# Second product and transposes over 64 rows at a time between the scores of places 2 and 3

## The chip, the cores and the metric

The kernel runs on one core of one Trainium2 chip. A core has a matrix engine (TensorE: PE, its weight loads are shown as PEld), a vector engine (VectorE: DVE), an activation engine (ScalarE: ACT), a general engine (GpSimd: POOL) and a queue for transfers (SyncE: SP). Each works through its own instructions in order, and they wait for each other by semaphores. TensorE reads from the on-chip memory SBUF and writes to PSUM, which here serves as 8 banks of 128 partitions by 512 fp32 numbers.

The metric is the device time of one execution in microseconds (us), as a median over several executions. The kernel before: 1874.29 us, the median of 3 runs (1870.79 to 1875.33).

## The reference

The input is `x`, 16 batches of 512 rows by 256 features, fp32. Each row is normalised to `xn`, and two branches are computed from it and multiplied:

```python
v  = xn @ v_w + v_b                                   # 16 heads of 16 features
scores = table[i - j] + qm[i] + km[j] + 0.15 * (qc[i] . kc[j]) / sqrt(8)   # per head, causal
ctx = softmax(scores) @ v
h   = layernorm(xn + ctx @ out_w + out_b)
s   = layernorm(h + gelu(h @ ffn_w1 + ffn_b1) @ ffn_w2 + ffn_b2)     # 256 -> 1024 -> 256
hid = silu(fp4(xn) @ fp4(w_gate).T) * (fp4(xn) @ fp4(w_up).T)        # 256 -> 704
g   = silu(fp4(hid) @ fp4(w_down).T)                                 # 704 -> 256
out = x + s * g
```

`fp4` rounds blocks of 16 numbers to a scale times one of eight magnitudes. `table` depends on the batch and the head and comes from a small network over the mean of `xn`.

## The kernel before, in words

Everything is fp32; the scores and two rows of biases are in the kind fp32r, which TensorE takes in one pass. An fp32 product appears in the profile as two instructions, each with a weight load of its own.

**Steps.** The main loop (L1112) has 64 steps: 16 batches, four groups of four heads each. The group is the *place* of a step within its batch, 0 to 3. At a step the kernel computes the attention weights of group g of batch b, and beside them a quarter of the rest of the previous batch ("old"): places 0 and 1 have the output product of the attention (`output`, L530) and the first normalisation, places 1 and 2 at their end the first product of the feed-forward network (`expand`, L592: for one half of the batch's rows, 8 blocks f), places 2 and 3 its second product (`contract`, L603) for the two halves. Each step also turns and multiplies one tile of 128 rows of the fp4 branch (`turned_x`, `hidden`, `turned_hidden`, `gate`), and places 3 and 0 project the batch that comes next.

**Scores.** For a group the scores are computed twice. `maxima` (L427) computes them with rows of the softmax on the partitions and VectorE takes the maximum of each row under the causal mask (tile names `ms`, `junk`, `mx`). One step later `weights` (L466) computes them turned, with the negated maxima as two further rows of the operand, and ScalarE takes `Exp` (names `ws`, `pr`); then POOL multiplies by the table (`tabled`, L494), and one step later still `context` (L502) multiplies by the values (name `cp`). Both kinds of scores have 36 or 38 rows to sum over. Two heads stand at partitions 0 and 64, and their products are issued in pairs, one over the lower 64 rows of TensorE and one over the upper 64 (`scores`, L413). A group's causal blocks come in five bursts (`BURSTS`, L281): of 512 columns per bank, and from the third on of 384 + 128, 384 + 128 and 256 + 256.

**Banks.** The 8 banks of PSUM are three pools: one bank for `cp`; one pair of banks, tag `ws`, for the weights of a burst and, later in the step, for the second half of the gated products (`gu`); and five banks, tag `mm`, for everything else, handed out by `bank(name)` (L246) and free again when their last reader has ended. A burst of maxima takes two of the five until VectorE has read them. A burst of weights takes the pair until ScalarE's `Exp` has read it; where the plan says V it takes two of the five instead.

**Order.** TensorE's order is the order of the program; VectorE's and ScalarE's too, from the main loop on (`fixed`, L1111). Within a step it is set by a string for each place, `PLAN` (L711). W and V are bursts of weights, M a burst of maxima on TensorE, `!` the reading of the outstanding maxima by VectorE together with whatever stands in the list `later`; a small letter takes the next piece of a generator: f two products (of 8 blocks of 128 features, for two tiles of 128 rows) of the second feed-forward product, x the transposes of a tile of `xn` after rounding, y those of the rounded hidden tile (six blocks, in two pieces), h those of a half of `h` for the next `expand`. At places 2 and 3 the strings are

```python
"WVM!ffWMM!ffxWM!ffWM!ffyyh", "WMV!ffWMM!ffxWM!fffWM!yfy"
```

After the string come `gp`, `up` (L657, two of the five banks), the transpose of the maxima (`mp`), `gu` on the pair, then at place 2 `gate` (`dp`) and `expand`, at place 3 the values of the next batch (`vp`) and `gate`. `context` of the next step follows.

**The pieces that the change touches.** `biased` (L285) starts an accumulation with the bias row: a product of ones with the row, 128 rows, two tiles of 256 columns. `contract` (L603) accumulates 2 x 8 products of 128 rows on it in one bank; when the last has been issued, `added` is put into `later`, by which VectorE adds the bank to `h` and takes the statistics. `turned_h` (L583), `turned_x` (L646) and `turned_hidden` (L683) turn blocks of 128 x 128 into banks of the five, and ScalarE copies them to SBUF.

Of the kernel before, what the change touches and what calls it, by code (L numbers as in the profile page):

```python
# [12 lines left out]
F32 = mybir.dt.float32  # L13
# [15 lines left out]
P = 128  # L29
# [21 lines left out]
def tile_block(ctx: ExitStack, tc: tile.TileContext, a: dict, pos: bass.AP, win: bass.AP, out: bass.AP):  # L51
# [230 lines left out]
        ((0, 0, 0),), ((1, 0, 0),), ((0, 1, 0), (0, 3, 384)), ((1, 1, 0), (1, 3, 384)), ((0, 2, 0), (1, 2, 256))  # L282
    )

    def biased(acc, i, tiles=2):  # L285

        mm(
            acc[:, : tiles * D].rearrange("p (t d) -> p t d", t=tiles), sums,
            rows[:, i, :].unsqueeze(1).to_broadcast([P, tiles, D]),
            start=True, stop=False, skip_group_check=True,  # L290
        )

    def rows_of(tiles, t):
# [228 lines left out]
    def added(h, tiles, acc, mv):  # L522
# [4 lines left out]
        for t in tiles:  # L527
            statistics(mv[:, t, :], rows_of(h, t))

    def output(b, h, cts, half, mv):  # L530

        cTs, ops = {}, []

        def normal(t):
            tp = bank(f"ctp_{b}_{t}").rearrange("p (h s) -> p h s", s=SLOT)
            for g in range(H // 4):
                turn(tp[:, 4 * g : 4 * g + 4, :].rearrange("p h s -> p (h s)"), cts[g][:, t * P : (t + 1) * P])
            rinv = sb.tile([P, H], F32, name=f"rinv_{b}_{t}", tag="rinv", bufs=2)
            dve.reciprocal(rinv, tp[:, :, HD])
            cx = sb.tile([P, H, HD], F32, name=f"cx_{b}_{t}", tag="cx", bufs=3)  # L540
            dve.tensor_tensor(cx, tp[:, :, 0:HD], rinv.unsqueeze(2).to_broadcast([P, H, HD]), ALU.mult)
            return cx.rearrange("p h d -> p (h d)")

        def turned(t, cx):
            t2 = bank(f"ct2_{b}_{t}")
            for c in range(NC):
                turn(t2[:, c * P : (c + 1) * P], cx[:, c * P : (c + 1) * P])
            cTs[t] = sb.tile([P, D], F32, name=f"cT_{b}_{t}", tag="cx", bufs=3)
            act.copy(cTs[t], t2[:, :D])

        def product(t):
            acc = bank(f"op_{b}_{t}")
            op = acc[:, :D]
            biased(acc, 0, 1)
            cT = cTs[t]
            for c in range(NC):
                mm(op, cT[:, c * P : (c + 1) * P], wo[:, c, :], start=False, stop=(c == NC - 1), skip_group_check=True)
            later.append(lambda: added(h, (t,), acc, mv))

        first, second = 2 * half, 2 * half + 1  # L560
        cx = normal(first)
        yield 0.43
        cx2 = normal(second)
        yield 0.43
        turned(first, cx)
        yield 0.21
        turned(second, cx2)
        yield 0.21
        product(first)
        yield 0.96  # L570
        product(second)
        yield 0.96
# [7 lines left out]
            layernorm(rows_of(h, t), mv[:, t, 0:1], rs[:, i : i + 1], g1, b1)  # L580
            yield

    def turned_h(b, h, half):  # L583
        hT = sb.tile([P, NC, 2 * P], F32, name=f"hT_{b}_{half}", tag="hT")
        tp = bank(f"htp_{b}_{half}")
        for c in range(NC):
            for t in range(2):
                turn(tp[:, (2 * c + t) * P : (2 * c + t + 1) * P], rows_of(h, 2 * half + t)[:, c * P : (c + 1) * P])
        act.copy(hT.rearrange("p c t -> p (c t)"), tp)
        return hT  # L590
# [9 lines left out]
            act.activation(acts[f], fp[:, : 2 * P], AF.Gelu, bias=fb1[:, f : f + 1])  # L600
        return acts

    def contract(b, h, half, acts, mv, together=2):  # L603

        for first in range(2 * half, 2 * half + 2, together):
            tiles = tuple(range(first, first + together))
            acc = bank(f"f2_{b}_{first}")
            biased(acc, 1, together)
            for i, t in enumerate(tiles):
                at = (t % 2) * P  # L610
                for f in range(NF):
                    mm(
                        acc[:, i * D : (i + 1) * D], acts[f][:, at : at + P], w2[:, f, :],
                        start=False, stop=(f == NF - 1), skip_group_check=True,
                    )
                    if t == tiles[-1] and f == NF - 1:
                        later.append(lambda tiles=tiles, acc=acc: added(h, tiles, acc, mv))
                    if f % 2:
                        yield 0.88

    def finish(b, h, half, mv, gated):

# [20 lines left out]
        src = xns[b][t // 2].rearrange("p t d -> p (t d)")  # L643
        return xq, fp4_stages(xq.rearrange("p t d -> p (t d)"), src, P, 2 * D)

    def turned_x(b, t, xq):  # L646
        xq = xq[:, t % 2, :]
        tp = bank(f"xqtp_{b}_{t}")
        for c in range(NC):
            turn(tp[:, c * P : (c + 1) * P], xq[:, c * P : (c + 1) * P])  # L650
        xqTs[b, t] = sb.tile([P, D], F32, name=f"xqT_{b}_{t}", tag="xqT")
        act.copy(xqTs[b, t], tp[:, :D])
        yield 0.21
# [26 lines left out]

        return hid, halves(), fp4_stages(hid[:, :I_FF], hid[:, :I_FF], P, I_FF, ROUNDING[t])

    def turned_hidden(b, t, hq):  # L683
        hqT = sb.tile([P, NI, P], F32, name=f"hqT_{b}_{t}", tag="hqT")
        for first, count in ((0, 4), (4, 2)):
            tp = bank(f"hqtp_{b}_{t}_{first}")
            for i in range(count):
                turn(tp[:, i * P : (i + 1) * P], hq[:, (first + i) * P : (first + i + 1) * P])
            act.copy(hqT[:, first : first + count, :].rearrange("p i t -> p (i t)"), tp[:, : count * P])
            hqTs[b, t] = hqT  # L690
            yield 0.43 if first == 0 else 0.21
# [16 lines left out]
        ("r|px|rpp|p|yyr", "pp"),  # L708
        ("p|x||yytt|tt", ""),
    )  # L710
    PLAN = ("WMc!llWM!xWM!ccllyWMlyW!M!l", "WMll!kWM!lWM!xllyhWMccy!WM!l", "WVM!ffWMM!ffxWM!ffWM!ffyyh", "WMV!ffWMM!ffxWM!fffWM!yfy")  # L711

    def keeping(b, g):
        kept(b, g)
        yield 0.0

    def turning_h(b, half):
        turned_hs[half] = turned_h(b, xns[b], half)
        yield 0.43

    def take(pieces, count):
# [390 lines left out]
    for s in range(STEPS):  # L1112
# [11 lines left out]
        if has_old:  # L1124
            if g % 2 == 0:
                mv = sb.tile([P, NT, 2], F32, name=f"mv{1 + g // 2}_{old}", tag=f"mv{1 + g // 2}")
            hand = {
                "c": coming,
                "l": output(old, xns[old], cts[:4], g, mv) if g < 2 else None,
                "k": keeping(b, 0) if g == 1 else None,  # L1130
                "f": contract(old, xns[old], g - 2, acts[g - 2], mv) if g > 1 else None,
                "x": turned_x(b, g, xqs[s // 2]),
                "y": turned_hidden(*before, hq),
                "h": turning_h(old, g - 1) if g in (1, 2) else None,
            }
            plan = PLAN[g].split("|")
        else:
            if g == 0:
                coming = project(1, x_second)
            hand = {  # L1140
                **first_hand, "c": coming, "x": turned_x(b, g, xqs[s // 2]),
                "y": turned_hidden(*before, hq) if g > 0 else None,
            }
            plan = FIRST_PLAN[g][0].split("|")
# [97 lines left out]
    for half in range(2):  # L1242
        acts[half] = expand(old, half, hT)
        if half == 0:
            hT = turned_h(old, h, 1)
        for i, _ in enumerate(contract(old, h, half, acts[half], mv, 1)):
            if i % 4 < 3:
                continue
            caught_up()
            t = 2 * half + i // 4  # L1250
            rs = sb.tile([P, 2], F32, name=f"rs_last_{t}", tag="rs2")
            inverse_deviation(rs[:, :1], mv[:, t : t + 1, 1])
            layernorm(rows_of(h, t), mv[:, t, 0:1], rs[:, :1], g2, b2)
# [47 lines left out]
```

## Time and profile before

| what | value |
|---|---|
| median of 3 runs | 1874.29 us |
| profiled execution: span from the first to the last instruction | 1872.6 us |
| PE busy / weight loads busy | 1774.8 / 1240.5 us (95% / 66%) |
| DVE, POOL, ACT busy | 1423.1, 1310.3, 1069.1 us (76%, 70%, 57%) |
| mean granted TensorE clock | 0.973 |
| instructions on PE | 10411 |

The page gives no other time of the profiled execution than its span; the median of the runs is 1.7 us above it. After the first two batches the steps repeat: each batch takes the same 106.1 us, 29.2 at place 2, 24.4 at place 3, 24.0 at place 0 and 28.5 at place 1.

"Busy" of PE counts each instruction from its start to a modelled end and includes what the engine needs between instructions. The chain of work that ended last gives each instruction only the time until the next link begins, so the price of a piece is better read there. Times such as 953.95 are microseconds from the start of the span; the batch quoted throughout runs from 922.48 (context at place 2) to 1028.60.

### The profile page before, as it was taken

The page shows a single profiled execution, that of the slowest core. Times are in us where ns is not written, and L with a number is a line of the kernel's source. Part 1 is how long each engine was busy: PE and PEld are TensorE (multiplying, and loading weights), DVE is VectorE, ACT ScalarE, POOL GpSimd, SP SyncE. Part 2 cuts the span into 40 slices and gives each one's busy share as a digit, 9 for nine tenths or more (in the row PEclk, how much of TensorE's full clock was granted, in tenths as well). Part 3 has the DMA queues.
Part 4 walks back from the last instruction along what each step waited for, and adds up shares of the span by engine and source line. Part 5 has one row for each costly group of instructions (what it writes and reads, how often), then busy time and mean ns, then how long its engine had stood idle before and what let it go on. Part 6 is the DMA issues. An engine that isn't in the chain of part 4 may idle for free.

```text
span 1872.6 us, 31762 instructions
## 1 busy us (share of the span) xinstructions
PE 1774.8 (95%) x10411; PEld 1240.5 (66%) x10411; DVE 1423.1 (76%) x3887; ACT 1069.1 (57%) x1853; POOL 1310.3 (70%) x1128
## 2 busy tenths in 40 slices
PE   5679799999999999999999999999999999999998
PEld 2235467676776767676776767677676767677676
DVE  5878587787878777787878777787878778787754
ACT  5654455655665555556565565556555565565553
POOL 5467477767776776777676776777677776777671
PEclk8869799999999999999999999999999999999999
DMA  6344242432323242422334242332333242232200
GB/s 203 95 148 134 81 129 68 138 87 88 109 89 120 68 126 80 137 84 76 112 95 127 60 135 81 117 101 76 112 94 109 73 138 86 77 108 79 72 21 12
DMA packets 127114, 184.68 MB, mean 99 GB/s; under 512 B 15315, under 2 KB 57749, under 8 KB 126949
## 3 DMA queue, kind: packets, MB, share of 16 engines
q1 hardware_dynamic: 122496, 181.25, 32.2%
q8 instruction: 83, 1.36, 0.3%
q10 hardware_dynamic: 4004, 0.98, 0.3%
q14 instruction: 83, 0.67, 0.1%
q0 software_dynamic: 448, 0.42, 0.1%
HBM read 136.45 MB, written 45.09 MB: 97 GB/s over the span
## 4 chain that ended last, share of the span: by engine, by line
PE 81%; DVE 8%; POOL 1%; issue 1%; ACT 1%; DMA 0%; DVEq 0%; POOLq 0%; ACTq 0%
PE f L72 25%; PE dp L72 8%; PE gu L72 8%; PE cp L72 7%; PE ws L72 5%; DVE junk L72 4%; PE op L72 4%; PE gp L72 4%; PE up L72 4%; PE ms L72 4%; PE vp L72 3%; PE hqtp L72 2%; DVE cx L72 1%; PE qk_wk L72 1%; PE qk_wq L72 1%
## 5 line engine op out<-in xcount | busy, mean ns | idle before, releaser
L500 POOL TENSOR_TENSOR pr<-pr,table 128x1024 f32<-128x1024 f32 (+2 forms) x448 | 768.0, 1748 | 75.2 <-ACT pr L72 73.0
L72 DVE CUSTOM_DVE_ANT_0 junk<-ms,mask 128x512 bf16<-128x512 f32 (+3 forms) x1024 | 501.9, 490 | 231.9 <-PE ms L72 155.0
L72 ACT ACTIVATE pr<-ws 128x1024 f32<-128x1024 f32 (+1 forms) x350 | 327.0, 955 | 134.4 <-PE ws L72 129.1
L72 ACT ACT_TABLE_LOAD x168 | 215.5, 1283 | 64.3 <-PE gp L72 48.8
L72 PE MATMUL f<-w,act 128*128 128x256 f32 x1024 | 249.0, 387 | 0.0
L72 PE MATMUL f<-hT,w 128*128 128x256 f32 x1024 | 226.3, 380 | 0.0
L72 PEld LDWEIGHTS f<-hT,w 128*128 128x128 f32 x1024 | 194.8, 190 | 26.3 <-ACT hT L72 0.2
L72 PEld LDWEIGHTS f<-w,act 128*128 128x128 f32 x1024 | 187.0, 190 | 31.3
L232 POOL TENSOR_TENSOR wide<-wide,scale 128x704 f32<-128x704 f32 (+1 forms) x71 | 96.6, 1361 | 136.5 <-DVE wide L72 132.9
L72 PE MATMUL ws<-qT,kT 38*128 38x512 f32 (+3 forms) x1024 | 157.5, 371 | 21.4 <-ACT pr L72 16.5
L72 PE MATMUL dp<-wdT,hqT 128*128 128x256 f32 x768 | 176.2, 379 | 0.0
L72 PEld LDWEIGHTS dp<-wdT,hqT 128*128 128x128 f32 x768 | 146.1, 190 | 31.1 <-issue 6.7
L72 ACT ACTIVATE act<-f,fb 128x256 f32<-128x256 f32 x256 | 118.2, 474 | 75.3 <-PE f L72 72.5
L72 PE MATMUL ms<-kT,qT 36*128 36x512 f32 (+3 forms) x1024 | 145.1, 330 | 9.5 <-DMA kT<-k_d 6.3
L72 PE MATMUL cp<-pr,va 128*17 128x512 f32 (+3 forms) x2048 | 151.5, 434 | 0.0
L72 PEld LDWEIGHTS ws<-qT,kT 38*128 38x128 f32 x1024 | 81.6, 188 | 90.8 <-issue 51.7
L72 PEld LDWEIGHTS cp<-pr,va 128*17 128x17 f32 x2048 | 54.3, 97 | 99.4 <-issue 79.5
L223 POOL TENSOR_SCALAR scale<-amax 128x32 f32<-128x32 f32 (+1 forms) x104 | 37.0, 356 | 116.6 <-DVE amax L72 113.5
L72 DVE TENSOR_TENSOR wide<-wide,m 128x704 f32<-128x704 f32 (+2 forms) x126 | 112.4, 892 | 4.1
L222 POOL TENSOR_TENSOR wide<-wide,inv 128x704 f32<-128x704 f32 (+1 forms) x71 | 99.1, 1396 | 21.5 <-DVE inv L72 21.1
L72 PEld LDWEIGHTS ms<-kT,qT 36*128 36x128 f32 x1024 | 96.2, 189 | 18.4 <-issue 12.8
L72 DVE TENSOR_SCALAR m<-m 128x512 f32<-128x512 f32 (+1 forms) x104 | 102.6, 986 | 3.4
(217 smaller groups left out, 3009.5 us busy)
## 6 DMA issues: line engine op xcount, KB each, us to landing
table<-rv SPq DMA_DIRECT2D x64, 1024.0 KB
kT<-k_d SPq DMA_DIRECT2D x256, 76.0 KB
qT<-q_d SPq DMA_DIRECT2D x256, 72.0 KB
x<-in_L_attn_x_dram SPq DMA_DIRECT2D x21, 512.0 KB
q_d<-q_hi SPq DMA_DIRECT2D x32, 256.0 KB
q_d<-q_lo SPq DMA_DIRECT2D x32, 256.0 KB
k_d<-k_hi SPq DMA_DIRECT2D x32, 256.0 KB
k_d<-k_lo SPq DMA_DIRECT2D x32, 256.0 KB
```

What stands on the lines that cost most here:

```text
L72: return lambda *args, **kw: self.follow(op(*args, **kw))
L222: nc.gpsimd.tensor_tensor(blocks(dst), blocks(src), per_block(inv), ALU.mult)
L223: nc.gpsimd.tensor_scalar(scale, amax, 1.0 / 6.0, 1e-12, ALU.mult, ALU.max)
L232: nc.gpsimd.tensor_tensor(blocks(dst), blocks(dst), per_block(scale), ALU.mult)
L500: nc.gpsimd.tensor_tensor(part, part, table[:, mine, j * P :], ALU.mult)
```

## The change

At places 2 and 3, from the second batch on (the first has strings and calls of its own, which stay):

- `contract` no longer sums over 128 rows in one bank. Each product becomes two, over the lower and the upper 64 rows, into two banks of the five; the bias row goes over 64 rows into the first of them. `f` is now one block (four products of the program's, twice two instructions of each) and there are 16 of them. `added_halves` adds both banks to `h`.
- x, y and h are turned by `by_halves`: each block of 128 x 128 as two blocks of 64 rows, the lower ones into one bank and the upper ones into the other of the pair `ws`; one copy by ScalarE puts both into the tile as it was before. y is one piece now instead of two.
- The strings of places 2 and 3 are new. V no longer appears there: all five bursts of weights use the pair. The first M comes behind the first transposes, y goes to the second part, h to the third, and the last part is `WM!` without f behind it.
- The product of the last batch, behind the loop, keeps its old form under the name `contract_tile`.

```diff
-    def biased(acc, i, tiles=2):
+    def biased(acc, i, tiles=2, n=P):
 
         mm(
-            acc[:, : tiles * D].rearrange("p (t d) -> p t d", t=tiles), sums,
-            rows[:, i, :].unsqueeze(1).to_broadcast([P, tiles, D]),
+            acc[:, : tiles * D].rearrange("p (t d) -> p t d", t=tiles), sums[:n],
+            rows[:n, i, :].unsqueeze(1).to_broadcast([n, tiles, D]),
             start=True, stop=False, skip_group_check=True,
         )
+
+    def by_halves(name, dst, blocks):
+
+        acc = ps_s.tile([P, 2, S], F32, name=name, tag="ws")
+        for i, src in enumerate(blocks):
+            for upper in range(2):
+                k = slice(64 * upper, 64 * upper + 64)
+                turn(acc[:, upper, i * 64 : (i + 1) * 64], src[k, :], ident[k, k])
+        n = len(blocks) * 64
+        act.copy(
+            dst.rearrange("p (i u t) -> p u i t", u=2, t=64), acc[:, :, :n].rearrange("p u (i t) -> p u i t", t=64)
+        )
...
+    def added_halves(h, half, acc, mv):
+
+        flat = h[half].rearrange("p t d -> p (t d)")
+        for part in acc:
+            dve.tensor_tensor(flat, part, flat, ALU.add)
+        for t in (2 * half, 2 * half + 1):
+            statistics(mv[:, t, :], rows_of(h, t))
...
-    def contract(b, h, half, acts, mv, together=2):
-
-        for first in range(2 * half, 2 * half + 2, together):
-            tiles = tuple(range(first, first + together))
-            acc = bank(f"f2_{b}_{first}")
-            biased(acc, 1, together)
-            for i, t in enumerate(tiles):
-                at = (t % 2) * P
-                for f in range(NF):
+    def contract(b, h, half, acts, mv):
+
+        tiles = (2 * half, 2 * half + 1)
+        acc = [bank(f"f2_{b}_{half}_{upper}") for upper in range(2)]
+        biased(acc[0], 1, 2, 64)
+        for i, t in enumerate(tiles):
+            for f in range(NF):
+                for upper in range(2):
+                    k = slice(64 * upper, 64 * upper + 64)
                     mm(
-                        acc[:, i * D : (i + 1) * D], acts[f][:, at : at + P], w2[:, f, :],
-                        start=False, stop=(f == NF - 1), skip_group_check=True,
+                        acc[upper][:, i * D : (i + 1) * D], acts[f][k, i * P : (i + 1) * P], w2[k, f, :],
+                        start=(upper == 1 and i == 0 and f == 0), stop=(f == NF - 1), skip_group_check=True,
                     )
-                    if t == tiles[-1] and f == NF - 1:
-                        later.append(lambda tiles=tiles, acc=acc: added(h, tiles, acc, mv))
-                    if f % 2:
-                        yield 0.88
+                if t == tiles[-1] and f == NF - 1:
+                    later.append(lambda: added_halves(h, half, acc, mv))
+                yield 0.44
...
-    def turned_x(b, t, xq):
+    def turned_x(b, t, xq, halves=False):
         xq = xq[:, t % 2, :]
+        if halves:
+            xqTs[b, t] = sb.tile([P, D], F32, name=f"xqT_{b}_{t}", tag="xqT")
+            by_halves(f"xqtp_{b}_{t}", xqTs[b, t], [xq[:, c * P : (c + 1) * P] for c in range(NC)])
+            yield 0.21
+            return
...
-    PLAN = ("WMc!llWM!xWM!ccllyWMlyW!M!l", "WMll!kWM!lWM!xllyhWMccy!WM!l", "WVM!ffWMM!ffxWM!ffWM!ffyyh", "WMV!ffWMM!ffxWM!fffWM!yfy")
+    PLAN = ("WMc!llWM!xWM!ccllyWMlyW!M!l", "WMll!kWM!lWM!xllyhWMccy!WM!l", "WfffxM!fWfffyM!ffWfffhM!ffWffMWM!", "WfffxM!fWfffyM!ffWfffM!fWfffMWM!")
...
-                "x": turned_x(b, g, xqs[s // 2]),
-                "y": turned_hidden(*before, hq),
+                "x": turned_x(b, g, xqs[s // 2], g > 1),
+                "y": turned_hidden(*before, hq, g > 1),
```

`turned_h` and `turned_hidden` get the same branch with four and six blocks; `turned_h` takes it for the second half of `h` only (the h of place 2).

## The prediction

> **What bounds the kernel now.** I read the busy shares first, then the chain that ended last, then one batch in the middle of the span.
>
> ```profile
> PE 1774.8 (95%) x10411; PEld 1240.5 (66%) x10411; DVE 1423.1 (76%) x3887; ACT 1069.1 (57%) x1853; POOL 1310.3 (70%) x1128
> ...
> PE 81%; DVE 8%; POOL 1%; issue 1%; ACT 1%; DMA 0%; DVEq 0%; POOLq 0%; ACTq 0%
> ```
>
> PE is the bound, so a microsecond off PE counts unless something else ends there instead. The four places of one batch, cut where the context products begin (places 2, 3, then 0, 1 of the next batch):
>
> ```profile
> 922.48:951.67 29.19, 29.19 (x172) 22.01 (x171) 23.39 (x59) 16.60 (x27) 21.84 (x19) 1.00 0.24 74
> 951.67:976.10 24.43, 24.43 (x151) 17.76 (x154) 16.57 (x50) 13.34 (x22) 19.12 (x16) 1.00 0.18 52
> 976.10:1000.15 24.05, 22.79 (x144) 14.75 (x147) 19.05 (x60) 14.64 (x24) 17.85 (x13) 1.00 0.40 124
> ```
>
> Columns: length, then busy PE, PEld, DVE, ACT, POOL, the clock, DMA. At places 2 and 3 PE never idles; at place 0 it does. How much of "busy" is work shows in the chain through place 3:
>
> ```profile
> 954.92 2.15 PE f L72 x9
> 957.08 0.43 PE ws L72 x4
> 957.51 0.53 PE ms L72 x5
> 958.03 1.92 PE f L72 x8
> 959.96 0.22 PE xqtp L72 x2
> 960.18 0.43 PE ws L72 x3
> 960.61 0.36 PE ms L72 x3
> 960.97 2.79 PE f L72 x12
> 963.76 0.43 PE ws L72 x2
> 964.19 0.24 PE ms L72 x3
> 964.43 0.59 PE hqtp L72 x4
> ```
>
> Long runs of f (6.91 us for 32 instructions in this chain) cost 0.216 each, transposes 0.11. Scores run as pairs, one in each half of the rows: in the timeline below a pair of 512 columns takes 0.23 (954.29 to 954.52), and both of a pair start together.
>
> ```profile
> 953.95 0.51 PE L72 MATMUL ws<-qT,kT 38*128 38x512 f32 x2
> 954.29 0.40 PE L72 MATMUL ms<-kT,qT 36*128 36x512 f32 x2
> 954.52 0.40 PE L72 MATMUL ws<-qT,kT 38*128 38x512 f32 x2
> ...
> 965.94 0.76 PE L72 MATMUL gp<-wgT,xqT 128*128 128x352 f32 x2
> ```
>
> From the first scores to gp: 965.94 - 953.95 = 11.99 us. Beside it VectorE reads the score banks (the lines show their start, length and idle time before them):
>
> ```profile
> 954.72 0.69 DVE L72 CUSTOM_DVE_ANT_0 junk<-ms,mask 128x512 bf16<-128x512 f32 x1 [1.91 <-PE ms L72]
> ...
> 960.57 0.56 DVE L72 CUSTOM_DVE_ANT_0 junk<-ms,mask 128x384 bf16<-128x384 f32 x1
> ...
> 961.61 0.56 DVE L72 CUSTOM_DVE_ANT_0 junk<-ms,mask 128x384 bf16<-128x384 f32 x1
> ```
>
> It starts 0.77 after the first scores and needs 1.04 for a bank of 384 + 128 columns (960.57 to 961.61).
>
> **What is removed: the changes between 128 and 64 rows.** Three of the four visits to 64 rows at place 3 vanish. Overhead = chain time of ws and ms, plus what the piece behind them takes over its plain price, less 0.23 per 512 columns. Second visit: 0.43 + 0.53 + (1.92 - 8 x 0.216) - 3 x 0.23 = 0.46. Third: 0.43 + 0.36 + (2.79 - 12 x 0.216) - 0.46 = 0.53. Fourth: 0.43 + 0.24 + (0.59 - 0.44) - 0.46 = 0.36. Together 1.35 us a place; 15 batches x 2 places: 40 us at the most.
>
> The Trainium skill (TensorEngine Tiling (Array Packing), Key Properties) says that changing the tiling mode drains the engine, which agrees with these 0.4 to 0.5 us. By that rule alone the sum would be -40 us.
>
> **What f becomes.** 32 instructions of 128 rows become 64 of 64 rows. No fp32 product over half the rows is in the trace. Lower bound: halves side by side like the score pairs, 32 slots of 0.216, no change. The context products, four side by side in fp32 (the view of places: 32 context products of up to 512 columns take 2.28 us of chain, and one by one, at 0.216 per 256 columns, they would take 8.64), say that fp32 doesn't forbid it. Upper bound: no overlap, 32 x 0.216 = +6.9 us a place. I take no change: both near rows run side by side. Transposes: two halves of 64 columns; the weight loads of a score pair go together, pair after pair 0.11 apart, so a block stays at 0.11 (bounds 0.05 and 0.22; at most ±0.1 x 12 blocks). More instructions to issue (f now has four loads and four products in 0.43): the context issues as many in 0.2 (953.18, 16 products in 0.83), so nothing. The bias row over 64 rows: same 512 columns, nothing.
>
> **The pair of banks.** Weights, x, y and h now share it; all five weights go through it (V is gone). ScalarE starts an Exp 0.6 us after the first scores and takes 1.02; free at about 1.65 after W. fff is 1.30, so x waits for nothing (the bias row stands ahead too), y and h 0.07 each; queued behind them is an M, and VectorE waits for that. Copies: 0.2 to start, 0.37 for 256 columns, 0.59 for 512, so some 0.81 for 768; behind x stand M and f (0.66), behind y M and ff (1.1): W waits up to 0.05. ScalarE is 57% busy. I count 0.1 us at place 3, 0.15 at place 2.
>
> **The five other banks: what is late next.** The second product now holds two of them from its first f until VectorE has added it, behind all maxima. The last part is M W M with nothing between but the weights: 2 + 2 + 2 = 6 banks of 5. So the fifth M's second bank waits for VectorE's first bank of the fourth M, and gp, next in PE's order, waits for the second one. Before, the last M pair was followed by ffyyh, 2 us of PE. Behind gp stand up, mp, gu, dp and the next place's context: all of PE moves with it.
> Place 3, time from W0: 0.34 first scores, 0.22 bias, 6.91 f, 0.22 x, 0.65 y, three W and four M at 0.23 or 0.27: 0.77 + 1.00. The fourth M ends at 10.1, with the waits 10.2. VectorE starts 0.20 later, reads two banks in 2.08, PE resumes 0.06 later (984.38 to 984.44, a transpose behind a maximum), and gp's weight load is uncovered (0.11): gp at 12.65 against 11.99, **+0.66**. Place 2: the same with h (0.43) and 0.15 of waits: fourth M ends 10.7, gp at 13.1 against 937.23 - 924.76 = 12.47, **+0.63**. VectorE is not ahead: the first M now stands behind fffx, so it starts at 2.5 instead of 0.77.
>
> The Trainium skill (TensorEngine Tiling (Array Packing), PSUM Pressure) speaks against the change here: row tiles write to different banks, so tiling takes more of them. Taken alone it turns the -40 us into a loss without giving its size.
>
> **VectorE behind it.** The fourth M's banks are read at 12.43, the fifth's, four reads of 0.47 to 0.54, at 14.4 (966.40 - 953.95 = 12.45 before). Then it adds two banks instead of one (0.69 each, the line at 966.33) and takes two statistics (1.13): the product with Silu starts at 17.0, before at 968.58, which is 14.63. From there its last add of place 3 ended 9.06 later (977.64), so now at 26.06. Place 0 begins at 24.39 + 0.66 = 25.05, and its first maximum could be read 0.76 behind that (978.34 to 979.10), at 25.81. VectorE is still busy then: 0.25, with the start of one more instruction **+0.3**, and it counts, because VectorE is the chain there (979.11 to 984.44). Bounds: 0 (the waits for POOL at 973.6 to 975.1 take the lag up) and 2.4, the whole lag. Behind place 2 the next first M comes 2.5 after W0: covered; were it not, it would be the same 2.4. POOL comes 1.4 later into place 0, and the end of its table products stands 7 us ahead of the context that reads them: covered. The maxima with their sign go to ScalarE, VectorE and, as mhi and mlo, by SP's queue into qT; 3 us later they still have some 7 us until the next W. None of the moved pieces (x, y, h, f, M) issues a DMA.
>
> **The first batch** has its own strings and keeps the old forms of x and y, and the product behind the loop keeps its form: nothing.
>
> **Sum.** 15 x (0.66 + 0.63) + 14 x 0.3 = 23.6 us on a profiled execution whose span is 1872.6: 1896.2. The median of the runs, 1874.29, is 1.7 above that span: 1898.
>
> **Rivals.**
> *Faster: gp isn't stopped.* If it and the last M find free banks, place 3 reaches gp at 10.2 + 0.46 + 0.3 = 10.95 (-1.0), place 2, where the last W waits for the fourth Exp, at 11.65 (-0.8): -28 us, 1846. It decides if gp starts under 1.8 us after the fourth M. For: PE is the bound everywhere else. Against: two banks at 1.04.
> *The lag grows.* VectorE's whole 2.4 us reach place 0, or half reaches 0 and half place 1: 14 x 2.1 more, 1928. For: VectorE leads at the start of both places (from 979.11 and 1003.71). Against: it waited for POOL 1.5 us at 973.6 and again at 997.5.
> *The change of rows stays*, as fp32 and fp32r don't mix: 1.35 a place comes back ahead of the fourth M, 30 x 1.35 = +40: 1940.
> *Halves don't overlap:* 30 x 6.9 = 207 on top: about 2105. Against: context and scores.
>
> **How the numbers follow.** Forecast 64% (1885 to 1913: ±0.25 for each of 30 places, and 0 to 0.8 at place 0), faster 16%, a balance within 0.3% (what a measurement of this kernel tells from no change, 5.6 us) 5%, growing lag 9%, rows stay 3%, no overlap 3%. The range 1866 to 1926 leaves out about 12% below and 8% above. Faster 0.16, same 0.05, slower 0.79.
>
> **What would show it.** Between W's at places 2 and 3 f at 0.216 per pair and no extra 0.2 around scores; PE idle ahead of gp, ended by a maximum (mx), 0.8 to 1.6 us, and within the fifth M; W0 to gp 12.6 and 13.1; places 2, 3, 0, 1 of 29.8, 25.1, 24.3 and 28.5 us. It is wrong if gp follows the fifth M at once, if f's pairs take over 0.23, or if W, x or y wait for Exp by more than 0.3 each.

## The result, and the profile after

The changed kernel takes 1921.24 us (median of 4 runs, 1919.39 to 1921.91) against 1873.97 us (4 runs, 1870.79 to 1875.33): 1.0252 times as long, with a 95% interval of 1.0238 to 1.0267. It is slower, as predicted, and the time lies inside the range, but it lost 47 us where the forecast said 24. About half of the loss is the one that was predicted; the other half was in no term of the sum.

The page of the kernel after, its busy times and the chain that ended last:

```profile
PE 1791.2 (93%) x11671; PEld 1259.1 (66%) x11671; DVE 1452.6 (76%) x3917; ACT 1072.5 (56%) x1793; POOL 1321.8 (69%) x1128
...
PE 78%; DVE 9%; ACT 3%; POOL 2%; issue 1%; DVEq 0%; POOLq 0%; ACTq 0%
```

PE has 16 us more of busy time in a span that grew by 47.5 (1872.6 to 1920.1), so its share falls. The granted clock says more: its mean fell from 0.973 to 0.956.

First three places in which the clock stayed full (places 2, 3, 0, cut as before where the context begins; length, then busy PE, PEld, DVE, ACT, POOL, the clock, DMA):

```profile
831.97:861.48 29.51, 28.57 (x216) 21.82 (x215) 21.72 (x57) 16.68 (x25) 21.05 (x18) 1.00 0.20 63
861.48:886.31 24.83, 23.70 (x187) 17.66 (x186) 19.07 (x53) 13.33 (x20) 18.67 (x16) 1.00 0.16 51
886.31:910.97 24.66, 23.56 (x140) 14.98 (x140) 19.87 (x57) 14.84 (x24) 19.30 (x15) 1.00 0.42 130
```

At places 2 and 3 PE was never idle before; now it idles 0.94 and 1.13 us. Taken as medians over places at full clock, the four places went from 29.17, 24.39, 24.02 and 28.5 to 29.5, 24.83, 24.67 and 28.5. That is 1.42 us a batch, some 21 us in all, where 1.59 a batch had been predicted.

The chain through place 3 of the batch that is quoted from here on:

```profile
979.10 0.50 PE hqtp L72 x12
979.60 0.29 PE ms L72 x2
979.89 0.87 PE f L72 x8
...
984.70 0.29 PE ms L72 x4
984.98 0.55 DVE junk L72
...
986.02 0.56 DVE junk L72
...
986.97 1.45 PE gp L72 x4
```

Eight instructions of f over half the rows cost 0.87, which is 0.217 a pair: halves run side by side. (A letter f is one block: two products of the program, one for each half of the rows, so four instructions.) What is new is that VectorE's reads of score banks stand in the chain. The timeline of PE shows where:

```profile
974.64 0.49 PE L72 MATMUL ws<-qT,kT 38*128 38x512 f32 x2
...
984.77 0.45 PE L72 MATMUL ws<-qT,kT 38*128 38x256 f32 x4
985.06 0.28 PE L72 MATMUL ms<-kT,qT 36*128 36x256 f32 x1
985.93 0.49 PE L72 MATMUL ms<-kT,qT 36*128 36x256 f32 x3 [0.59 <-DVE mx L72]
986.97 1.45 PE L72 MATMUL gp<-wgT,xqT 128*128 128x352 f32 x4 [0.55 <-DVE mx L72]
```

The fifth M stops after its first product for a bank, and gp behind it stops again, both until VectorE has read a maximum (mx). From the first scores, 974.64, to gp are 12.33 us; before, 11.99.

The timeline of VectorE at place 3 and at the start of place 0:

```profile
977.10 0.69 DVE L72 CUSTOM_DVE_ANT_0 junk<-ms,mask 128x512 bf16<-128x512 f32 x1 [2.19 <-PE ms L72]
...
984.97 0.56 DVE L72 CUSTOM_DVE_ANT_0 junk<-ms,mask 128x384 bf16<-128x384 f32 x1 [0.37 <-PE ms L72]
...
988.92 1.41 DVE L72 TENSOR_TENSOR xn<-f,xn 128x512 f32<-128x512 f32 x2
...
1000.09 0.89 DVE L72 TENSOR_TENSOR wide<-wide,m 128x704 f32<-128x704 f32 x1
1000.89 0.68 DVE L72 CUSTOM_DVE_ANT_0 junk<-ms,mask 128x512 bf16<-128x512 f32 x1
```

Its first read comes 2.46 after the first scores, it adds two banks in place of one, and at place 0 it goes from its last operation for the batch before (1000.09) to the first maximum without idle time. Before, that maximum had 1.46 us of idle time ahead of it:

```profile
979.10 0.69 DVE L72 CUSTOM_DVE_ANT_0 junk<-ms,mask 128x512 bf16<-128x512 f32 x1 [1.46 <-PE ms L72]
```

**What no term foresaw** stands in two stretches of 3.413 us at place 2 (the third number from the end is the clock):

```profile
952.76:956.17 3.41, 2.47 (x25) 1.78 (x21) 2.59 (x12) 2.51 (x3) 2.89 (x4) 1.00 0.11 30
956.17:959.58 3.41, 3.41 (x6) 2.12 (x7) 3.08 (x11) 1.29 (x2) 2.73 (x2) 0.50 0.30 96
```

In the first, PE waits twice for banks ahead of gp. In the second its clock is halved, for exactly 3.413 us, and only six instructions of PE begin in it. The whole place, 941.09 to 972.36, takes 31.27 instead of 29.51. The clock record holds 3 single windows of this kind in the steady batches before, all at place 1, and 19 after (longer stretches of low clock, which both kernels have in their first and last batches, aren't counted, here and below). What one costs is the length of its place less that of the same place at full clock:

| place | windows before | windows after | us each | us more |
|---|---|---|---|---|
| 2 | 0 | 5 | 31.2 - 29.5 = 1.7 | 8.5 |
| 3 | 0 | 3 | 26.5 - 24.8 = 1.7 | 5.1 |
| 0 | 0 | 4 | 25.3 - 24.7 = 0.6 | 2.4 |
| 1 | 3 | 7 | 30.0 - 28.5 = 1.5 | 6.0 |

That is 22 us. With the 21 of the places it gives 43; from the beginning of the second batch's steps to the last context, the trace of after is 42.5 us longer (1700.79 against 1658.30). Of the 5 us that are left, 1.8 lie ahead of this and 3.2 behind it, and were not followed up. The sums are a little generous: behind each halved place 3, place 0 took 24.02 to 24.39 instead of 24.67, since VectorE had caught up meanwhile.

### The profile page after: what moved, and what is told of

Read it like the earlier page. It is cut to its first block, busy times and chain, and to the rows that moved or that the text cites. A ratio compares the mean times of both kernels' runs of the same rounds, so it can differ in the third digit from the quotient of the medians.

```text
span 1920.1 us, 34294 instructions
## 1 busy us (share of the span) xinstructions
PE 1791.2 (93%) x11671; PEld 1259.1 (66%) x11671; DVE 1452.6 (76%) x3917; ACT 1072.5 (56%) x1793; POOL 1321.8 (69%) x1128
## 4 chain that ended last, share of the span: by engine, by line
PE 78%; DVE 9%; ACT 3%; POOL 2%; issue 1%; DVEq 0%; POOLq 0%; ACTq 0%
PE f L72 23%; PE dp L72 8%; PE gu L72 8%; PE cp L72 7%; DVE junk L72 5%; PE gp L72 5%; PE op L72 4%; PE up L72 4%; PE ws L72 4%; PE ms L72 3%; PE vp L72 3%; PE hqtp L72 2%; ACT pr L72 1%; PE qk_wk L72 1%; PE qk_wq L72 1%
## 5 line engine op out<-in xcount | busy, mean ns | idle before, releaser
L72 ACT ACTIVATE pr<-ws 128x1024 f32<-128x1024 f32 x320 | 328.2, 1026 | 127.3 <-PE ws L72 113.0
L72 PE MATMUL f<-w,act 64*128 64x256 f32 (+1 forms) x1984 | 270.9, 380 | 0.0
L72 PEld LDWEIGHTS f<-w,act 64*128 64x128 f32 (+1 forms) x1984 | 201.2, 187 | 16.7
L72 PE MATMUL ms<-kT,qT 36*128 36x512 f32 (+3 forms) x1024 | 179.4, 360 | 25.7 <-DVE mx L72 14.7
L72 PE MATMUL ws<-qT,kT 38*128 38x512 f32 (+3 forms) x1024 | 165.1, 380 | 14.0 <-ACT pr L72 8.0
L72 PEld LDWEIGHTS ms<-kT,qT 36*128 36x128 f32 x1024 | 109.2, 191 | 44.5 <-DVE mx L72 23.2
L72 PEld LDWEIGHTS ws<-qT,kT 38*128 38x128 f32 x1024 | 85.1, 188 | 72.9 <-ACT pr L72 28.7
L72 DVE SCALAR_TENSOR_TENSOR xn<-xn,rs,b 128x256 f32<-128x256 f32 x124 | 88.4, 713 | 33.7 <-POOL rs L114 28.4
```

The source lines that it names most:

```text
L72: return lambda *args, **kw: self.follow(op(*args, **kw))
```

## The experiments

Three things could make the loss, and the profile names all of them: the wait for banks ahead of gp (**banks**), VectorE's second addition with its late start (**VectorE**), and the halved **clock** behind the waits. The rival to all three is that the half-row form itself costs more than it saves. Each edit below is against the kernel after, if nothing else is said.

### Work put into the waits

```diff
-"WfffxM!fWfffyM!ffWfffhM!ffWffMWM!", "WfffxM!fWfffyM!ffWfffM!fWfffMWM!"
+"WfffxM!fWfffyM!ffWfffhM!ffWffMWZMZ!", "WfffxM!fWfffyM!ffWfffM!fWfffMWZMZ!"
...
+            elif letter == "Z":
+                for i in range(2):
+                    mm(cp[:, :D], w2[:64, i, :P], w2[:64, i, :], start=True, stop=True, skip_group_check=True)
```

Z is two products that nobody reads, put where PE idles.

> The changed kernel with four further products per place 2 and 3: two (lower 64 rows, 256 columns, into the bank of the context products, read by nobody) ahead of the fifth M and two ahead of gp, where PE waits. Work is added and nothing is taken away. Theory A (the waits of 0.87 and 0.82 us make PE idle enough that the clock is halved in the next 3.41 us window; 8 such windows in places 2 and 3 of the profile after, 1.7 us each): the products run inside the waits, gp starts within 0.1 us of where it did, the halved windows at places 2 and 3 disappear, and the time falls by 8 to 14 us, to about 1909. Those at places 0 and 1 stay or move. Rival B (the halved windows have nothing to do with the waits, or cost nothing): the time stays or rises by 30 x 0.1 = 3 us. Rival C (PE is not waiting there but working): it rises by 30 x 1.7 = 52 us.

Measured: 1911.35 us (1908.05 to 1920.6), 1.0202 [1.0174, 1.023] times the kernel before, so some 10 us less than without the added work, although places 2 and 3 became longer: 29.84 and 24.98. Views of places 2, 3 and, two rows on, place 1:

```profile
944.27:974.11 29.84, 29.84 (x224) 22.90 (x223) 21.67 (x57) 16.70 (x25) 21.22 (x18) 1.00 0.18 60
974.11:999.09 24.98, 24.98 (x196) 18.87 (x195) 19.08 (x53) 13.33 (x20) 18.82 (x16) 1.00 0.17 56
...
1023.63:1053.73 30.10, 29.55 (x181) 21.64 (x180) 25.45 (x69) 17.96 (x31) 19.69 (x16) 0.94 0.50 142
```

No idle time is left at places 2 and 3, and in the steady batches no window at these places is halved any more (8 in the kernel after). The edit adds work and takes away nothing but idleness, so the clock follows what PE does in these waits; whether it follows the idle time itself or the work done, the run can't tell. A kinder position of the windows isn't the reason: seven of them began 11.98 to 12.28 us into place 3, and in the kernel after and in the one with a short addition (below) every window that began between 11.42 and 12.31 was followed by a halved one. What spoils the gain is in the third row: in the profiled run, at 1920.6 the longest of the four, place 1 was halved in 12 batches. A batch of this kernel takes about 109.3 us, and 32 windows of 3.413 are 109.23, so once a window lies badly at a place, it does so in batch after batch.

### M ahead of f

```diff
-"WfffxM!fWfffyM!ffWfffhM!ffWffMWM!", "WfffxM!fWfffyM!ffWfffM!fWfffMWM!"
+"WM!fffxfWM!fffyffWM!ffhffWM!ffWM!f", "WM!fffxfWM!fffyffWM!fffWM!ffWM!ff"
```

Each M stands right behind its W again, with f behind the last one, so that VectorE has read the banks when gp comes.

> The changed kernel with other strings alone: M directly behind each W, and f behind the last M: WM!fffxfWM!fffyffWM!ffhffWM!ffWM!f and WM!fffxfWM!fffyffWM!fffWM!ffWM!ff. Products, transposes, banks and instruction counts stay. Theory A (the base loss is the order: VectorE starts 2.5 us after W0 and gp waits for its banks; row halves themselves save about 1 us a place): VectorE starts at 0.8, gp is at 11.2 to 11.5 after W0 at place 3 and 11.7 to 12 at place 2 (before: 11.99 and 12.47), place 0 loses nothing, the halved windows fall back to about four: 1845 to 1855, faster than before. Rival B (halves are slower in themselves, through the pair of banks or the products): gp stays where the pair's waits put it, 1900 to 1920.

Measured: 1872.75 us, 0.9988 [0.9978, 0.9997]. The whole loss is gone by order alone. Places 2 and 3:

```profile
918.31:947.03 28.72, 28.62 (x215) 21.16 (x214) 21.55 (x57) 16.69 (x25) 21.20 (x18) 1.00 0.18 52
947.03:970.93 23.90, 23.83 (x187) 17.25 (x186) 19.07 (x53) 13.34 (x20) 18.91 (x16) 1.00 0.21 70
```

The waits ahead of gp are gone, 11.91 and 11.42 us from the first scores at places 2 and 3, both under those of the kernel before (12.47 and 11.99), and the steady batches hold four halved windows instead of 19. The time expected was missed by some 20 us, though: the bank waits end, but the M's are spaced with the W's, so VectorE is still late, and place 0 stays at 24.5 with its first maximum read 1.25 us behind its first scores (0.76 before the change, 1.42 after).

### Without the upper half's addition

```diff
-        for part in acc:
-            dve.tensor_tensor(flat, part, flat, ALU.add)
+        dve.tensor_tensor(flat, acc[0], flat, ALU.add)
```

> The changed kernel, but VectorE adds only the lower half's bank to h (left out: the upper 64 rows of the second product are not added, so h is a different one). One VectorE instruction of 0.69 us less at places 2 and 3. Theory A (place 0 is 0.65 us longer than before because VectorE comes late out of place 3): place 0 gets 0.4 to 0.65 shorter, places 2 and 3 stay within 0.1, since the add stands behind all reads that PE waits for; 6 to 10 us in all, and up to 2 us more if the four halved windows of place 0 go too. Rival B (VectorE's lag is made up before place 0 and its loss has another cause): within 2 us of the changed kernel.

Measured: 1887.52 us, 1.0067 [1.005, 1.0084], which is 34 us less than after; 6 to 12 had been expected. The miss has a plain cause. A bank that nobody reads comes free with its last product, so the edit took away not only an addition but one of the two banks that f holds. The timeline of PE at place 3:

```profile
968.87 0.41 PE L72 MATMUL ms<-kT,qT 36*128 36x256 f32 x4
969.73 1.45 PE L72 MATMUL gp<-wgT,xqT 128*128 128x352 f32 x4 [0.46 <-DVE mx L72]
...
972.87 0.28 PE L72 MATMUL mp<-ident,mx 128*16 128x128 f32 x1 [0.50 <-DVE mx L72]
```

The fifth M runs through in one piece and gp waits once; then the transpose of the maxima (mp) waits, since VectorE hasn't finished. Places 2 and 3 fall to 29.13 and 24.45, 0.38 less each, and the steady batches hold 4 halved windows instead of 19, none at these places. So this run speaks for the banks, but can't price the addition.

### A short addition that keeps its bank

```diff
-        for part in acc:
-            dve.tensor_tensor(flat, part, flat, ALU.add)
+        dve.tensor_tensor(flat, acc[0], flat, ALU.add)
+        dve.tensor_tensor(flat[:, :8], acc[1][:, :8], flat[:, :8], ALU.add)
```

> The changed kernel, but of the upper half's bank VectorE adds only the first 8 of 512 columns (left out: the rest of the upper 64 rows of the second product). Unlike in the run with one add, that bank still has a reader behind all maxima, so it is held as long; only VectorE's time falls, by about 0.6 a place. Theory A (in the run with one add the unread bank came free for the fifth M and gp, which took 0.4 off places 2 and 3; the add itself costs only place 0): gp stays at 12.76 and 12.33 after W0, places 2 and 3 stay within 0.1 at full clock, place 0 falls from 24.7 to about 24.2: 6 to 12 us less than the changed kernel, about 1910. Rival B (it was the 0.69 of VectorE): as fast as the run with one add, 1888.

Measured: 1914.4 us, 1.0219 [1.0204, 1.0234], 7 us less than after. The bank has a reader again and the waits are back, gp at 12.68 and 12.32. Places 2, 3 and 0 of one batch:

```profile
829.42:858.92 29.50, 28.55 (x216) 21.74 (x215) 21.54 (x57) 16.68 (x25) 21.08 (x19) 1.00 0.20 68
858.92:883.75 24.83, 23.70 (x187) 17.71 (x186) 18.23 (x52) 13.32 (x20) 19.18 (x16) 1.00 0.15 49
883.75:907.91 24.16, 22.85 (x141) 14.72 (x140) 19.89 (x57) 14.62 (x24) 18.80 (x15) 1.00 0.40 128
```

Places 2 and 3 don't move; place 0 falls from 24.66 to 24.16. So the second addition costs its 0.5 to 0.6 us at place 0 and nowhere else, and the rest of what the run without it gained is the bank's: the 0.38 us at each of places 2 and 3, and the halved windows there, of which this trace has twelve (14 in all). Half of VectorE's theory holds.

### The same order without half rows

Against the kernel before:

```diff
-"WVM!ffWMM!ffxWM!ffWM!ffyyh", "WMV!ffWMM!ffxWM!fffWM!yfy"
+"WM!ffxWM!ffyyWM!ffhWM!fWM!f", "WM!ffxWM!ffyyWM!ffWM!fWM!f"
```

> The kernel before (128 rows, one bank, transposes in banks of the five) with strings in the order of the M-first run: WM!ffxWM!ffyyWM!ffhWM!fWM!f and WM!ffxWM!ffyyWM!ffWM!fWM!f. Tells the order from the rows. Theory A (changes of rows cost 0.36 to 0.53 a visit): five visits a place instead of four, and the fifth W waits for an Exp: +0.4 to +1.0 a place, 1885 to 1905. Rival B (the gain of the M-first run, if there is one, comes from the order alone): as fast as that run, below 1870.

Measured: 1897.11 us, 1.0117 [1.0102, 1.0132]; places 29.5, 24.74, 24.03, 28.5. This asks whether the order alone, with M behind every W, would have helped the old form as it helped the new one. It made it slower, by 0.33 and 0.35 us at places 2 and 3, a little under the 0.4 that had been expected at least; the time came into the range with the help of the clock, 7 halved windows against 3. So what M ahead of f won over the kernel after isn't a gain that the order brings everywhere.

### M early

```diff
-"WfffxM!fWfffyM!ffWfffhM!ffWffMWM!", "WfffxM!fWfffyM!ffWfffM!fWfffMWM!"
+"WM!fffxM!fWfffM!yffWM!fffhM!fWfffW", "WM!fffxM!fWfffM!yffWM!fffWM!fffWf"
```

The M's run ahead of the W's, and the last W has no M behind it.

> The changed kernel with strings in which M runs ahead of the weights: WM!fffxM!fWfffM!yffWM!fffhM!fWfffW at place 2 and WM!fffxM!fWfffM!yffWM!fffWM!fffWf at place 3. The five M stand at about 0.3, 2.1, 4.3, 6.3 and 8.2 us after W0 (in the M-first run 0.3, 3.3, 6.6, 9.4, 11.1), so that VectorE ends the maxima at 10.9 and has added both banks by 12.3; gp finds its banks free. Theory A (in the M-first run VectorE, still late by the spacing of M, kept places 3 and 0 from gaining): gp at 10.6 to 11.1, place 2 about 27.9, place 3 about 23.2, place 0 24.0 to 24.4, few halved windows: 1835 to 1850, faster than before. Rival B (the second add and the pair of banks eat what the rows save): no better than the M-first run, 1865 to 1880.

Measured: 1856.89 us (1848.24 to 1861.48), 0.9902 [0.9882, 0.9921]: about 1% faster than the kernel before. Places 2, 3, 0, 1, and place 1 of the next batch:

```profile
918.11:946.30 28.19, 28.16 (x216) 21.46 (x215) 23.75 (x58) 16.57 (x25) 21.43 (x19) 1.00 0.12 41
946.30:969.63 23.33, 23.30 (x187) 17.37 (x186) 19.23 (x52) 13.33 (x20) 18.62 (x16) 1.00 0.27 86
969.63:993.79 24.16, 22.85 (x141) 14.71 (x140) 19.90 (x57) 14.64 (x24) 18.80 (x15) 1.00 0.43 130
993.79:1022.32 28.53, 27.98 (x181) 20.38 (x180) 25.06 (x69) 17.88 (x31) 19.62 (x16) 1.00 0.48 152
1098.05:1128.11 30.06, 29.51 (x180) 21.42 (x179) 25.38 (x68) 17.97 (x31) 19.71 (x16) 0.94 0.48 144
```

Places 2 and 3 are 0.98 and 1.06 us shorter than before the change, and gp comes at 11.37 and 10.82, which is what the prediction's faster rival gave for PE without a wait (11.65 and 10.95). So the half-row form does save what the changes of rows cost; only the strings of the change didn't let it. The last row shows what is left: 9 of the steady places 1 have a halved window, 1.5 us each. That this is also why the runs spread over 13 us fits their mean clocks, 0.974 in the fastest and 0.966 in the slowest, but only one of them has a trace.

### Which part of the half rows pays

Two edits of the kernel with M early. The first turns x, y and h whole, in banks of the five as before (its strings have yy in place of y):

```diff
-        turned_hs[half] = turned_h(b, xns[b], half, half == 1)
+        turned_hs[half] = turned_h(b, xns[b], half)
...
-                "x": turned_x(b, g, xqs[s // 2], g > 1),
-                "y": turned_hidden(*before, hq, g > 1),
+                "x": turned_x(b, g, xqs[s // 2]),
+                "y": turned_hidden(*before, hq),
```

> The M-early run with x, y and h turned whole, over 128 rows, in banks of the five (y in two pieces, one behind the other), as before the change; the second product stays in halves. Theory A (each visit to 128 rows between scores costs 0.36 to 0.53): three more visits at place 2 and two at place 3, 15 x 5 x 0.45 = 34 us more, less some waits of W for copies from the pair: 1880 to 1895. Rival B (it is enough to take f over 64 rows): within 5 us of the M-early run.

Measured: 1903.23 us, 1.0152 [1.0136, 1.0167]; places 2 and 3 29.83 and 24.70, so 1.64 and 1.37 more. Three visits to the transposes at place 2 and two at place 3 cost 0.55 to 0.69 each, more than the 0.36 to 0.53 read from the trace before, and the time expected was passed by 8 us. But the whole blocks also hold banks of the five again, and the second piece of y waits for one, here at place 2:

```profile
942.07 0.44 PE L72 MATMUL hqtp<-ident,wide 128*128 128x128 f32 x2 [0.40 <-DVE mx L72]
```

At place 3 the same wait is 0.36. Without it the visits cost (1.64 - 0.40) / 3 = 0.41 and (1.37 - 0.36) / 2 = 0.50, as read before.

The second leaves the transposes in halves and sums f over all 128 rows in one bank:

```diff
-        acc = [bank(f"f2_{b}_{half}_{upper}") for upper in range(2)]
-        biased(acc[0], 1, 2, 64)
+        acc = bank(f"f2_{b}_{half}")
+        biased(acc, 1, 2)
...
-                for upper in range(2):
-                    k = slice(64 * upper, 64 * upper + 64)
-                    mm(
-                        acc[upper][:, i * D : (i + 1) * D], acts[f][k, i * P : (i + 1) * P], w2[k, f, :],
-                        start=(upper == 1 and i == 0 and f == 0), stop=(f == NF - 1), skip_group_check=True,
-                    )
+                mm(
+                    acc[:, i * D : (i + 1) * D], acts[f][:, i * P : (i + 1) * P], w2[:, f, :],
+                    start=False, stop=(f == NF - 1), skip_group_check=True,
+                )
...
-                    later.append(lambda: added_halves(h, half, acc, mv))
+                    later.append(lambda: added(h, tiles, acc, mv))
```

> The M-early run with the second product whole again: 128 rows, one bank, one add by VectorE, one block per f; the transposes stay in halves in the pair of banks. Theory A (changes of rows): seven stretches of f a place, each with a change there and back where the M-early run has one, so 30 x 6 x 0.45 = 81 us more, less 30 x up to 0.3 for the add and the bank that are saved: 1920 to 1945. Rival B (the gain over the kernel before comes from VectorE and the order, not from the rows): 1850 to 1880.

Measured: 1921.57 us, 1.0249 [1.0232, 1.0267]. Places 2 and 1:

```profile
941.04:971.09 30.05, 30.05 (x183) 21.13 (x182) 24.02 (x57) 16.55 (x25) 21.70 (x19) 1.00 0.13 41
...
1020.26:1050.27 30.01, 29.47 (x180) 21.59 (x180) 25.20 (x67) 17.85 (x31) 19.26 (x15) 0.94 0.47 142
```

Place 2 takes 1.87 more and place 3 1.82 more; about 2.7 had been expected. The time is right for another reason: a batch takes 109.23 us, 32 windows again, and every steady place 1 is halved, 7.3 to 7.4 us into it. With these strings either part alone gives up what both together save: the change of rows is paid wherever one kind of 128-row work is left between the scores.

### Place 1

Two edits of the kernel with M early that touch only place 1, to ask whether the halved windows there go with the idle time. First, one product of 128 rows that nobody reads at each of two waits:

```diff
-"WMll!kWM!lWM!xllyhWMccy!WM!l"
+"WMll!kWM!ZlWM!xZllyhWMccy!WM!l"
...
+            elif letter == "Z":
+                mm(cp[:, :D], w2[:, 0, :P], w2[:, 0, :], start=True, stop=True, skip_group_check=True)
```

> The M-early run with two further products per place 1 (128 rows, 256 columns, 0.43 us each, into the bank of the context products after it has been copied; read by nobody), each ahead of a transposed context tile (ct) for which PE waits 0.4 to 0.5 us. In the M-early run 9 of the 13 steady places 1 had a halved clock and took 30.1 instead of 28.5 us. Theory A (idle of PE in a window of the clock's monitor halves the next window): place 1 takes 28.5 to 28.7 everywhere, 9 x 1.5 = 13 us less, 1838 to 1848. Rival B (the halving follows from something else, such as the load of the array): place 1 keeps halved windows, 1857 or more.

Measured: 1850.02 us (1849.27 to 1850.54), 0.9868 [0.9853, 0.9882]. Place 1 has no idle time left and takes 28.7 in the steady batches (once 29.05), with no halved window in any:

```profile
985.67:1014.37 28.70, 28.70 (x184) 21.21 (x184) 25.05 (x69) 17.85 (x31) 19.62 (x16) 1.00 0.49 151
```

The position of the windows isn't the reason here either: four began 4.05 to 4.59 us into the place, and in M early every one that began between 3.92 and 4.63 was followed by a halved one.

Second, x and y one part earlier, so that work of the place fills the waits:

```diff
-"WMll!kWM!lWM!xllyhWMccy!WM!l"
+"WMll!kWM!xlWM!yllhWMccy!WM!l"
```

> The M-early run with work of its own, instead of idle products, in the two holes of place 1: x ahead of the first ct and the first y ahead of the second ct (WMll!kWM!xlWM!yllhWMccy!WM!l). Nothing is added. Theory A (idle of PE in one window of the monitor halves the next; the holes are 0.4 to 0.5 us each): place 1 takes 27.7 to 28.3 us everywhere, no halved windows in steady places 1: 1838 to 1848, the fastest of all. Rival B (what is moved only moves the wait behind it): place 1 stays at 28.5 and keeps halved windows, 1850 to 1860.

Measured: 1848.41 us (1847.8 to 1849.2), 0.9856 [0.9842, 0.9869], the fastest of all, 27 us under the kernel before the change on the same chip (1875.9) and some 73 under the changed one. One batch of it, places 2, 3, 0, 1:

```profile
908.10:936.30 28.20, 28.17 (x216) 21.52 (x215) 23.79 (x59) 16.50 (x25) 21.41 (x19) 1.00 0.12 40
936.30:959.63 23.33, 23.30 (x187) 17.40 (x186) 19.21 (x52) 13.37 (x21) 18.61 (x16) 1.00 0.28 87
959.63:983.77 24.14, 22.84 (x141) 14.73 (x140) 19.90 (x57) 14.63 (x24) 18.78 (x15) 1.00 0.43 130
983.77:1012.28 28.51, 28.04 (x181) 20.35 (x180) 25.08 (x68) 17.96 (x31) 19.65 (x16) 1.00 0.49 152
```

I had hoped for place 1 to get shorter; at 28.51 it didn't. The gain over M early is in the clock: 2 halved places 1 in place of 9. The windows ahead of them still hold 0.3 us of idle time, where M early has 0.55.

Last, the same filling as above in the kernel before the change:

```diff
-"WMll!kWM!lWM!xllyhWMccy!WM!l"
+"WMll!kWM!ZlWM!xZllyhWMccy!WM!l"
...
```

> The kernel before with the two idle products of 0.43 us per place 1, ahead of the transposed context tiles. In its profile 3 of the steady places 1 had a halved window, at 1.5 us each, and the products cost 0.2 us each place 1 (28.7 for 28.5 in the M-early run with them). Theory A (the gate follows idle time, and in the kernel before its windows are rare because batches of 106.1 us do not line up with windows of 3.41): 3 x 1.5 - 15 x 0.2, within 0.3% of the kernel before, with no halved window at places 1. Rival B (the gain of the filled M-early run came from the products in another way): 5 us or more faster.

Measured: 1876.28 us, 1.0005 [0.9996, 1.0014]. Its 3 halved windows went too, some 4.5 us, and place 1 went from 28.5 to 28.7, some 3 us the other way. The two would make it 1.5 us faster, which the medians don't show; why was not followed up. Filling pays only where the clock is lost often.

## Why the prediction was right, and where it fell short

- **gp waits for banks** (+0.66 and +0.63). Right in its mechanism and place: the idle time ahead of gp and within the fifth M is there, ended by a maximum, and goes when the order leaves VectorE time (M ahead of f, M early), or in part when f holds one bank less (without the upper half's addition). The size was half of what was said: +0.34 and +0.29. At place 3 the fourth M ended at 10.13, said 10.2. Then 0.20 until VectorE starts, 1.94 for its two banks instead of 2.08, and 0.06 until PE resumes; no 0.11 for the weight load showed.
- **f's 32 slots of 0.216.** Right, 0.217 a pair. The transposes were cheaper than 0.11 a block: y's twelve half blocks take 0.50 of the chain, against 0.65 for six whole ones. The rival that halves don't overlap falls with it.
- **The changes of rows removed** (1.35 a place). Right, and so the rival that they stay falls: with the wait gone, M early gains 0.98 and 1.06 a place on the kernel before, near the 0.8 and 1.0 of the prediction's faster rival, and whole transposes cost it 0.41 to 0.50 a visit beside a wait for a bank.
- **VectorE's lag at place 0** (+0.3). Right in kind, but 0.65. It started the product with Silu at 16.8 (said 17.0) and freed itself 26.25 after the first scores of place 3 (said 26.06). Place 3 was 0.2 shorter than said, counted to the first scores of place 0, so that less of the lag was covered: the sum had taken an error on one side of a race as harmless. The short addition shows that 0.5 to 0.6 of it is the second bank's addition. The growing lag as a rival is not what happened: place 1 stayed at 28.5 at full clock.
- **Waits of W, x and y for Exp** (0.1 to 0.15). Of no weight, as said: the waits of ws for pr fell from 16.5 us in all to 8.0.
- **The sum of these.** The places lost 1.42 us a batch where 1.59 had been said. That this is near is partly luck: the two waits were half of what was said and the lag twice.
- **The missing term.** The sum priced idle time at its own length. Sixteen more halved windows added 22 us. The page of before showed 0.973 as mean clock, and its trace three halved windows at place 1, each behind idle time of PE; I had not asked what they cost. No rival named it, and the range held the time only because it had been made wide for the lag and the changes of rows; that is luck. The time fell near the growing lag's 1928 for a reason that isn't the lag.

Whether the half rows are worth having was the wrong question to settle from the strings that came with them: the same code with other strings at places 1, 2 and 3 is 1.4% faster than before.

## What to carry to other kernels

Count the banks that each piece holds at the tightest place, with the reader that frees them, and give the engine that waits for the bank other work while the last reader reads; a reordering that saves engine time gives it back there otherwise. Price a new idle gap on TensorE not only at its length, but also at a chance of a halved window of the clock behind it (here 1.5 to 1.7 us where PE is the bound, behind windows with 0.3 to 1.1 of idle time). If a kernel's runs spread or added work makes it faster, look at the granted clock window by window.

## What the runs showed of the hardware

- The clock is granted in windows of 3.413 us on a fixed grid (in each trace its changes lie on the grid within 0.004 us); in the steady batches it was either full or 0.5. The Trainium skill (TensorE: Matmul & The Clock Gate, Part 1: The HAM clock gate) gives 3413 ns and a free-running window, which agrees.
- The same page (Part 1 and HAM oscillation) has the clock fall after a whole idle window and warns of gaps over about 3.4 us; its section on a second failure mode adds that very short idle times can do it too when they are frequent, without a length. Here windows were halved behind ones in which PE idled 0.3 us in all (M early with x and y one part earlier), 0.5 to 0.7 (places 0 and 1) and 0.9 to 1.1 (places 2 and 3), and filling the gaps with products ended it at places 1, 2 and 3. The measurement decides: a third of the 3.413 us, and less, is enough.
- Idle time doesn't decide alone. In the steady batches of all the traces no window was halved behind one with less than 0.29 us of it, but many with more stayed without effect. At place 3 of the kernel after, thirteen windows held 1.05 to 1.13 us of idle time; the three that began 12.18 to 12.31 us into the place were followed by a halved one, the four that began at 11.11 to 11.30 and the six at 12.36 to 12.77 were not. The kernel with the short addition agrees: behind all nine windows that began at 11.42 to 12.30 the clock was halved, behind the five at 11.26 and at 12.47 to 12.77 it wasn't. So where the grid falls on the work decides, and what the gate counts within a window stays open.
- A batch whose length is a whole number of windows keeps its place on the grid. At 109.23 us, 32 windows, the kernel with whole f had every steady place 1 halved; at 107.52 us, 63 windows in two batches, the old form in the new order had every second one.
- Products over 64 rows in fp32 run two at a time at the price of one over 128 (0.217 a pair of 64 x 256), and transposes over halves cost less than whole ones (0.50 for twelve halves against 0.65 for six blocks).
